# Q and K of a group as one product of 2x4 by 4x4 blocks with 26 multiplications, and every engine's order from a list schedule

## The chip, the cores and the metric

The kernel runs on one NeuronCore of a Trainium2 chip. The metric is the device time of one execution in microseconds (us), as the median of several runs. The kernel before takes 1929.07 us (three runs, 1928.95 to 1929.9).

In the profile the engines are called PE (matrix products), PEld (its weight loads), DVE (VectorE), ACT (ScalarE), POOL (GpSimd) and SP (which only issues DMAs). Matrix products land in PSUM, eight banks of 128 partitions by 512 fp32 values; everything else is in SBUF or in device memory.

## The reference

All data is fp32. There are 128 batches of 128 nodes with 512 features, and two layers:

```python
# layer 0: adj stands for W1 and W2, so C - A is the bias alone
A   = adj @ x                                    # per batch
x   = layernorm(x + max over features of relu(A + b))
# layer 1: eight-head attention, masked where adj == 0
q, k, v = split(x @ w_qkv)                       # 8 heads of 64
attn = softmax(where(adj == 0, -inf, q @ k.T / 8))
o   = (attn @ v) @ w_proj + b_proj
x   = layernorm(x + o + layernorm(o) * gamma + beta)
```

## The kernel before, in words

The 128 batches go in 32 groups of four, so a group has 512 tokens of 512 features. One group after the other passes through these stages, and three or four groups are in work at once:

- Layer 0: `l0_mm` makes adj @ x per batch (one 128x512 product), `l0_max` takes the largest value of each row on DVE, `l0_add` (L302, ACT) adds it to x, `bn` and `finish_stats` make mean and deviation (DVE and POOL), `l0_norm` normalizes (ACT). The result is transposed through a DVE transpose and two DMAs into `x1T`. `l0_beta` (POOL, 128x1024) adds beta and `l0_spill` writes x out for the last residual.
- Q, K and V of a group, and later the projection O, each by Strassen's method. A `Unit` (L163) cuts the 512 tokens and the 512 features into two halves each and makes seven products of half blocks. A product is four matmuls of 128x256. The sums of weight blocks are made once at the start; the four sums of token blocks (`left_sums`, L211) are made per group on POOL, 128x512 each, and `x_sums` (L372) shares one set between Q, K and V. A group has two units for Q and K (`qk_unit`, L378), one for V and one for O: 28 products, 112 matmuls of 128x256.
- Within a unit, products are summed in PSUM where they can be: `snap` (L185, ACT) copies a bank to SBUF, `relay` (L190, ACT) copies a bank into another bank, and `result` (L203, DVE) adds a bank and a copy into the output. Per group that makes, with Q and K alone, six ACT copies and eight DVE additions of 128x512.
- Attention per batch: `scores` (PE), the mask (`softmax_mask`, DVE), the row maximum (`softmax_max`, DVE), eight exponentials (`softmax_exp`, ACT), the division by the row sum (`softmax_div`, L450, one DVE TENSOR_TENSOR of 128x1024 with two inputs in SBUF), a DVE transpose (`pu`), two DMA steps to the transposed probabilities `pT`, and `attend` (PE), copied by ACT to `oT`.
- The tail of a group: `tail_bias` adds the bias to o (POOL, 128x1024), then mean and deviation of o, normalization (ACT), times gamma, plus o, plus x (`tail_inner`, `tail_residual`: three POOL operations of 128x1024 per two batches), mean and deviation again, the last normalization (ACT), and the store.

The order of the work on every engine is the order in which the program issues it (`pin`), written out by hand: PE works on one group's unit while DVE, ACT and POOL prepare the next, and the two units of Q and K, V and O are interleaved product by product so that there is always another product to run while a bank is being copied. Memory comes from pools with two to four buffers to a name.

The lines that matter below are these. L75 is the helper of all matmuls, L78 that of every TENSOR_TENSOR, on DVE and on POOL; L187 is the copy of `snap`; L274 and L276 are in `finish_stats`, L300 in `l0_max`, L418 the mask, L434 the row maximum, L441 the exponentials, L462 the transpose of probabilities, L692 a last normalization on DVE. In the tile names of the page `b_qk`, `b_v`, `b_o` are PSUM banks of the units, `u_qk` and so on the copies, `s_x` and `s_o` the token sums.

Of the kernel before, what the change touches and what calls it, by code (L numbers as in the profile page):

```python
# [1 line left out]

# [7 lines left out]
F32 = mybir.dt.float32  # L10
AF = mybir.ActivationFunctionType
ALU = mybir.AluOpType
AX = mybir.AxisListType


@with_exitstack
def kernel(
# [12 lines left out]

# [6 lines left out]
    GT = G * P  # L55
    HT = GT // 2
    HE = D // 2
    NG = B // G
    NP = H // 2
    Q = 4  # L60
    QS = P // Q
    LA = 10
# [3 lines left out]
    const = ctx.enter_context(tc.tile_pool(name="const", bufs=1))  # L66
    sb = ctx.enter_context(tc.tile_pool(name="sb", bufs=1))
    small = ctx.enter_context(tc.tile_pool(name="small", bufs=4))
    dram = ctx.enter_context(tc.tile_pool(name="dram", bufs=3, space=bass.MemoryType.DRAM))
    psum = ctx.enter_context(tc.tile_pool(name="psum", bufs=1, space=bass.MemoryType.PSUM))  # L70

    pin = tc.keep_in_program_order

    def pe(*args, **kwargs):
        pin(nc.tensor.matmul(*args, **kwargs))  # L75
# [3 lines left out]

    zeros = const.tile([P, 2 * P], F32, name="zeros")
    pin(nc.vector.memset(zeros, 0.0))
    idle = psum.tile([P, 2 * P], F32, tag="b1", name="idle")

    def keep_warm(n):
        for _ in range(n):
            pe(idle, lhsT=zeros[:, :P], rhs=zeros, start=True, stop=True)

    adj_sb = const.tile([P, P], F32, name="adj_sb")  # L90
    pin(nc.sync.dma_start(out=adj_sb, in_=adj))
    bias0 = const.tile([P, 1], F32, name="bias0")
    pin(nc.sync.dma_start(out=bias0, in_=l0_b.unsqueeze(1)))

    def broadcast(queue, name, src):
        t = const.tile([P, D], F32, name=name)
        pin(queue.dma_start(out=t, in_=src.partition_broadcast(P)))
        return t
# [3 lines left out]
    xs, pairs = {}, {}  # L102

    def load(q, *queues):
        tag, bufs = ("o", 3) if 2 <= q <= 4 else ("x", 2)
        pairs[q] = t = sb.tile([P, 2, D], F32, tag=tag, name=f"x_{q}", bufs=bufs)
        for j, queue in enumerate(queues):
            pin(queue.dma_start(out=t[:, j], in_=x[2 * q + j]))
        if not queues:
            pin(nc.sync.dma_start(out=t, in_=x[ds(2 * q, 2)].rearrange("j p d -> p j d")))  # L110
        for j in range(2):
            xs[2 * q + j] = t[:, j]
# [3 lines left out]
    def weight_load(w, src, col1, col2, cols, width):  # L116
        rows = src.rearrange("(d c p) e -> d p c e", d=2, p=P)
        for i, d, col in ((0, 0, col1), (3, 0, col2), (1, 1, col1), (2, 1, col2)):
            pin(
                nc.sync.dma_start(  # L120
                    out=w[:, i, :, ds(cols, width)], in_=rows[d, :, :, ds(col + cols, width)]
                )
            )

    def weight_sums(w, cols, width, *steps):
        t = w[:, :, :, ds(cols, width)]
        b11, b21, b22, b12 = (t[:, i] for i in range(4))
        sums = ((4, b12, b11), (6, b22, b12), (5, b22, t[:, 4]), (3, b21, t[:, 5]))
        for i, left, right in {(): sums, (1,): sums[:1], (2,): sums[1:3], (3,): sums[3:]}[steps]:
            tt(nc.gpsimd, t[:, i], left, right, ALU.subtract)  # L130

    WQK = [P, 7, 2, D]
    wqk = sb.tile(WQK, F32, tag="wqk", name="wqk")
    wv = const.tile([P, 7, 2, HE], F32, name="wv")
    wp = const.tile([P, 7, 2, HE], F32, name="wp")

    load(0, nc.scalar, nc.scalar)
    load(1, nc.sync, nc.sync)
    be_bc = broadcast(nc.scalar, "be_bc", ln_beta)
    weight_load(wqk, w_qkv, 0, D, 0, HE)  # L140
    load(2)
    weight_load(wqk, w_qkv, 0, D, HE, HE)
    load(3)

    warm = small.tile([P, 1], F32, tag="r", name="warm")
    pin(nc.scalar.activation(warm, zeros[:, :1], AF.Identity, bias=zeros[:, :1]))
    keep_warm(3)
    ident = const.tile([P, P], F32, name="ident")
    make_identity(nc, ident)
    mhalf = const.tile([P, 1], F32, name="mhalf")  # L150
    pin(nc.gpsimd.memset(mhalf, -0.5))
# [3 lines left out]
    adjT = const.tile([P, P], F32, name="adjT")  # L155
    pt0 = psum.tile([P, P], F32, tag="po", name="pt0")
    pin(nc.tensor.transpose(pt0, adj_sb, ident))
    pin(nc.vector.tensor_copy(adjT, pt0))
    mask = const.tile([P, P], F32, name="mask")
    pin(nc.vector.tensor_scalar(mask, adj_sb, 0.0, -3.0e38, ALU.is_equal, ALU.mult))  # L160


    class Unit:  # L163

        def __init__(self, name, lefts, mm, out):
            self.name, self.lefts, self.mm, self.out = name, lefts, mm, out
            self.banks, self.snaps = {}, {}  # L170

        def product(self, i):
            bank = {1: 1, 6: 1, 7: 1, 2: 2, 5: 3, 3: 3, 4: 4}[i]
            first = bank not in self.banks
            if first:
                self.new_bank(bank)
            self.mm(self.banks[bank], i - 1, self.lefts[i], first)

        def new_bank(self, bank):
            self.banks[bank] = psum.tile(  # L180
                [P, 2, HT], F32, tag=f"b{bank}", name=f"b{bank}_{self.name}"
            )
            return self.banks[bank]

        def snap(self, k):  # L185
            t = sb.tile([P, 2, HT], F32, tag=f"u{k}", name=f"u{k}_{self.name}")
            pin(nc.scalar.copy(t, self.banks[1]))  # L187
            self.snaps[k] = t

        def relay(self):  # L190

            pin(nc.scalar.copy(self.new_bank(2), self.banks[1]))

        def relayed(self):
            for dst, src in self.places(0, 0, self.banks[2]):
                pin(nc.scalar.copy(dst, src))

        def places(self, half, col, bank):

            out = self.out[half, col]  # L200
            return [(d, bank[:, k]) for k, d in enumerate(out)] if type(out) is list else [(out, bank)]

        def result(self, half, col):  # L203
            bank, k = {(0, 0): (2, 1), (0, 1): (3, 2), (1, 0): (4, 3), (1, 1): (3, 3)}[half, col]
            adds = zip(
                self.places(half, col, self.banks[bank]), self.places(half, col, self.snaps[k])
            )
            for (dst, a), (_, b) in adds:
                tt(nc.vector, dst, a, b, ALU.add)

    def left_sums(name, a11, a12, a21, a22):  # L211
        s = [
            sb.tile([P, 2, HT], F32, tag=f"{name[0]}s{k}", name=f"s{k}_{name}") for k in range(1, 5)
        ]
        return dict(zip((1, 2, 3, 4, 5, 6, 7), (a11, a12, s[3], a22, s[0], s[1], s[2]))), (
            (s[0], a21, a22, ALU.add),
            (s[1], s[0], a11, ALU.subtract),
            (s[2], a11, a21, ALU.subtract),
            (s[3], a12, s[1], ALU.subtract),
        )  # L220

    def run_sums(sums, eng=None):
        for dst, a, b, op in sums:
            tt(eng or nc.gpsimd, dst, a, b, op)

    def weight_stationary(w, cols):
        def mm(bank, i, left, first):
            for k in range(2):
                for c in range(2):
                    pe(  # L230
                        bank[:, k],
                        lhsT=w[:, i, c, ds(cols + k * P, P)],
                        rhs=left[:, c],
                        start=first and k == 0 and c == 0,
                        stop=True,
                        skip_group_check=True,
                    )

        return mm

    def tokens_stationary(w):
        def mm(bank, i, left, first):
            for k in range(2):
                for c in range(2):
                    pe(
                        bank[:, k],
                        lhsT=left[:, c, ts(k, P)],
                        rhs=w[:, i, c],
                        start=first and k == 0 and c == 0,
                        stop=True,  # L250
                        skip_group_check=True,
                    )

        return mm


    NC = 6
    stat_of = {}

    def bn(src, mv, k):  # L260
        st = small.tile([P, 6], F32, tag="st", name=f"st_{k}_{mv.name}")
        pin(nc.vector.bn_stats(st, src))
        pin(nc.vector.bn_aggr(mv[:, k], st))  # L263

    def finish_stats(mv, keys, fused=0):


        n = len(keys)
        if n == 0:
            return  # L270
        part = slice(fused, n)
        sh = small.tile([P, NC], F32, tag="sh", name=f"sh_{mv.name}")
        if n > fused:
            pin(nc.vector.tensor_scalar(sh[:, part], mv[:, part, 0], -1.0, None, ALU.mult))  # L274
# [1054 lines left out]
```

## Time and profile before

| | |
|---|---|
| median of three runs | 1929.07 us |
| span of the profiled execution | 1927.6 us, 1.5 us under the median |
| PE busy | 1915.8 us, 99% of the span |
| DVE busy | 1591.0 us, 83% |
| POOL busy | 1289.5 us, 67% |
| ACT busy | 1054.4 us, 55% |
| device memory | 176 GB/s over the span, DMA engines about two thirds busy |
| period of a group, from the chain of waits | 59.39 us (the same piece begins at 941.09 and 1000.48 us) |

The page gives the busy time of each engine, then the span in 40 slices, then the chain of work that ended last, then groups of equal instructions with the mean duration of one, and the idle time of the engine ahead of them. The timeline lists single instructions: start, duration, engine, line, output and inputs, shape. Its duration of an instruction contains the time that it is held up after it was issued, so that the same instruction can have several durations.

### The profile page before, as it was taken

To read this page: it belongs to the slowest core of one execution; us is meant where nothing else is said; L and a number is where in the kernel's file an instruction comes from. 1 tells how busy PE (TensorE), PEld (TensorE's weight loads), DVE (VectorE), ACT (ScalarE), POOL (GpSimd) and SP (SyncE) were. 2 spreads that over 40 slices of the span, in tenths; PEclk is the share of its full clock that TensorE was granted. 3 is DMA by queue.
4 is the path that set the end of the run, shared out by engine and by line. 5 is a ranking of instruction groups with operands and counts; after the bars stand their busy time and mean duration, and the time that the engine had idled before them with its cause. 6 is when DMAs were issued, how large, how long until landed. Compare 5 with 4: busy or idle time off the path is not lost.

```text
span 1927.6 us, 33369 instructions
## 1 busy us (share of the span) xinstructions
PE 1915.8 (99%) x11539; PEld 1637.9 (85%) x11539; DVE 1591.0 (83%) x2516; ACT 1054.4 (55%) x3093; POOL 1289.5 (67%) x826
## 2 busy tenths in 40 slices
PE   9999999999999999999999999999999999999998
PEld 7888888888888888888888888888888888888885
DVE  6868888888888888888888888888888888888888
ACT  3444655645555556555465564555555655546476
POOL 6444766768667676676676676766767667677658
PEclk9999999999999999999999999999999999999999
DMA  7746667666676666766667756667666676666665
GB/s 228 179 127 165 162 186 191 164 183 158 181 203 158 186 164 180 203 162 178 169 179 189 179 169 180 162 187 198 162 187 158 182 206 158 181 165 182 170 196 177
DMA packets 444936, 341.76 MB, mean 177 GB/s; under 512 B 276832, under 2 KB 378336, under 8 KB 444768
## 3 DMA queue, kind: packets, MB, share of 16 engines
q1 hardware_dynamic: 444336, 338.85, 65.9%
q8 instruction: 91, 1.49, 0.3%
q10 hardware_dynamic: 432, 0.79, 0.1%
q14 instruction: 77, 0.63, 0.1%
HBM read 172.82 MB, written 166.72 MB: 176 GB/s over the span
## 4 chain that ended last, share of the span: by engine, by line
PE 97%; POOL 1%; DMA 1%; DVE 1%; ACT 0%; issue 0%; SPq 0%; POOLq 0%; ACTq 0%
PE b_qk L75 40%; PE b_o L75 19%; PE b_v L75 19%; PE pss L75 6%; PE po L75 6%; PE pa L75 6%; POOL zl L78 0%; DMA x<-in_x_dram 0%; DMA pT<-hop 0%; DVE s L78 0%; POOL rs_mv_last L78 0%; ACT s L441 0%; DMA hop<-pu 0%; PE idle L75 0%; DVE pu L462 0%
## 5 line engine op out<-in xcount | busy, mean ns | idle before, releaser
L75 PE MATMUL b_qk<-s_x,wqk 128*128 128x256 f32 x2048 | 472.8, 379 | 0.0
L75 PEld LDWEIGHTS b_qk<-s_x,wqk 128*128 128x128 f32 x2048 | 389.0, 190 | 53.5 <-DVE xt L323 0.2
L441 ACT ACTIVATE s<-s,nmax 128x128 f32<-128x128 f32 x1008 | 390.2, 391 | 4.5 <-DVE nmax L434 4.5
L75 PE MATMUL b_qk<-x1T,wqk 128*128 128x256 f32 x1536 | 360.5, 381 | 0.1
L276 POOL TENSOR_SCALAR rs_mv<-mv 128x6 f32<-128x6 f32 (+2 forms) x61 | 14.7, 241 | 501.2 <-DVE mv L263 501.2
L75 PEld LDWEIGHTS b_qk<-x1T,wqk 128*128 128x128 f32 x1536 | 289.3, 190 | 43.1 <-issue 1.0
L78 DVE TENSOR_TENSOR s<-s,rec 128x1024 f32<-128x1024 f32 x126 | 282.5, 2242 | 4.3
L78 DVE TENSOR_TENSOR qk<-b_qk,u_qk 128x512 f32<-128x512 f32 x256 | 170.3, 687 | 137.0 <-ACT u_qk L187 83.7
L187 ACT COPY u_qk<-b_qk 128x512 f32<-128x512 f32 x192 | 112.5, 586 | 276.9 <-PE b_qk L75 275.3
L75 PE MATMUL b_v<-wv,s_x 128*128 128x256 f32 x1024 | 236.9, 379 | 0.1
L75 PE MATMUL b_o<-wp,s_o 128*128 128x256 f32 x992 | 229.3, 379 | 0.0
L418 DVE SCALAR_TENSOR_TENSOR s<-pss,mask 128x512 f32<-128x512 f32 x252 | 156.2, 682 | 78.5 <-PE pss L75 78.4
L75 PEld LDWEIGHTS b_v<-wv,s_x 128*128 128x128 f32 x1024 | 194.4, 190 | 27.0 <-DVE qk L78 0.5
L75 PEld LDWEIGHTS b_o<-wp,s_o 128*128 128x128 f32 x992 | 188.3, 190 | 25.8 <-POOL zl L78 0.2
L78 POOL TENSOR_TENSOR z<-z,ga_bc 128x1024 f32<-128x1024 f32 x58 | 162.8, 2807 | 51.0 <-ACT z L285 51.0
L441 ACT ACTIVATION_READ_ACCUMULATOR s<-s,nmax 128x1 f32 x1008 | 190.7, 189 | 0.0
L187 ACT COPY u_v<-b_v 128x512 f32<-128x512 f32 x95 | 55.6, 585 | 246.2 <-PE b_v L75 242.8
L187 ACT COPY u_o<-b_o 128x512 f32<-128x512 f32 x91 | 53.3, 586 | 250.2 <-PE b_o L75 250.2
L78 POOL TENSOR_TENSOR x<-x,be_bc 128x1024 f32<-128x1024 f32 x64 | 178.3, 2787 | 17.5 <-DVE xt L323 16.2
L75 PE MATMUL b_v<-wv,x1T 128*128 128x256 f32 x768 | 176.5, 379 | 0.0
L75 PEld LDWEIGHTS b_v<-wv,x1T 128*128 128x128 f32 x768 | 145.8, 190 | 32.3 <-issue 13.9
L75 PE MATMUL b_o<-wp,oT 128*128 128x256 f32 x744 | 171.1, 379 | 0.0
(142 smaller groups left out, 3305.7 us busy)
## 6 DMA issues: line engine op xcount, KB each, us to landing
hop<-pu SPq DMA_DIRECT2D x128, 512.0 KB, 3.1
pT<-hop SPq DMA_DIRECT2D x512, 128.0 KB, 3.8
spill<-x SPq DMA_DIRECT2D x64, 512.0 KB, 5.2
x<-in_x_dram SPq DMA_DIRECT2D x62, 512.0 KB, 4.5
xhop<-xt SPq DMA_DIRECT2D x248, 128.0 KB, 2.3
x1T<-xhop SPq DMA_DIRECT2D x248, 128.0 KB, 3.9
xr<-spill SPq DMA_DIRECT2D x59, 512.0 KB, 3.6
out_dram<-xr SPq DMA_DIRECT2D x58, 512.0 KB, 4.5
```

The lines of the kernel that those rows point to most:

```text
L75: pin(nc.tensor.matmul(*args, **kwargs))
L78: pin(eng.tensor_tensor(dst, a, b, op))
L187: pin(nc.scalar.copy(t, self.banks[1]))
L276: pin(nc.gpsimd.tensor_scalar(rs[:, :n], mv[:, :n, 1], EPS, None, ALU.add))
L418: nc.vector.scalar_tensor_tensor(s[:, par], pss[b][par], SCALE, mask.unsqueeze(1).to_broadcast([P, NP, P]), ALU.mult, ALU.add,)
L441: nc.scalar.activation(prob[b][:, i], prob[b][:, i], AF.Exp, bias=nmax[b][:, i : i + 1], accum_out=psums[b][:, i : i + 1],)
```

## The change

The change rewrites the program around a planner. What it does:

- Q and K of a group become one product. The tokens are cut into 2 by 4 blocks (two batches of 128 tokens each, by 128 features), the weights of Q and K into 4 by 4 blocks (128 features by 256 outputs). 26 products, each of one 128x256 token block (a sum or a plain block) and one of 26 weight blocks, take the place of the 14 products of half blocks. A product is now two matmuls of 128x256, so a group has 52 instead of 56. The first group makes Q and K plainly with 64 matmuls from the weights as they are.
- The token blocks: 18 sums of 128x256 per group on POOL (`token_sums`). V makes its four sums of 128x512 itself.
- The outputs: a table `NODES` gives for each of 26 steps which product goes into which of eight banks, into which other banks the bank is copied by ACT (`seeds`), whether it is copied to SBUF by ACT for later additions (`adds`), and which of the eight outputs it ends. Per group there are 18 ACT copies of 128x512 for Q and K, eight DVE operations that write the outputs, two DVE additions in PSUM and two POOL additions of 128x512.
- The weight blocks for Q and K are made at the start, by 39 additions of 128x256 on DVE and POOL and six ACT operations.
- `tail_bias` is gone: ACT puts the bias into the banks of O ahead of its products (two copies of 128x512 per group). `l0_add` is gone: the row's constant goes into the shift of the normalization (`finish`, on POOL).
- The division of the softmax is no longer one DVE operation with two inputs. It is eight operations of 128x128 per batch, with a column of reciprocals as pointer scalar: on ACT for batches 0 and 2 of a group, on DVE for batches 1 and 3 (TENSOR_SCALAR).
- V's product 3 (`closing`) comes after O's products 1 and 2, O's product 3 after the third step of Q and K; both add to a bank out of which DVE must have taken `result(1, 1)`.
- Most buffers are single. PE's order is the order in which the program adds the work; the order on DVE, ACT, POOL and SP comes from `Plan.run`, a list schedule over costs written into the program: whenever an engine is free, of the operations that are ready the one that is due first.
- The last group's projection, residual and normalization are written anew with POOL for one half and DVE for the other.

The core of the diff. The change takes these out (of the functions above `qk_unit`, `x_sums`, `left_sums`, `tail_bias`, `l0_add` and the written-out order of the groups go as well):

```diff
-    def softmax_div(b):
-        rec = small.tile([P, H], F32, tag="rec", name=f"rec_{b}")
-        pin(nc.vector.reciprocal(rec, psums.pop(b)))
-        p = prob[b]
-        tt(nc.vector, p, p, rec.unsqueeze(2).to_broadcast([P, H, P]), ALU.mult)
```

It puts these in:

```diff
+NODES = [
+    (((8, 0),), 0, 3, (2,), (), None),
+    (((12, 1),), 2, 6, (), (19,), None),
+    (((14, 2),), 1, 4, (8,), (), None),
+    (((1, 3), (10, 4)), 0, 5, (), (7,), None),
...
+    (((2, 25),), 0, None, (), (), 0),
+]
...
+    def run(self, lead):
...
+            while coming[e] and coming[e][0][0] <= now + 1e-9:
+                _, n, op = heapq.heappop(coming[e])
+                heapq.heappush(ready[e], (op.due, n, op))
+            _, _, op = heapq.heappop(ready[e])
+            op.start = now
+            free[e] = now + op.cost
...
+    def token_sums(g):
...
+        for n, (a, b, s) in enumerate(SUMS):
...
+            plan.add(
+                "POOL",
+                0.74,
+                lambda t=t, c=c, pa=pa, pb=pb, s=s: tt(
+                    GP, t.t[:, c], pa(), pb(), ALU.add if s > 0 else ALU.subtract
+                ),
+                [(ba, ka), (bb, kb)],
+                [(t, c)],
+            )
...
+    def qk_unit(g, phys, between=()):
...
+        for n, (prods, lb, chain, seeds, adds, block_) in enumerate(NODES):
...
+            for tok, w in prods:
...
+                def emit(b=b, w=w, ap=ap, fresh=fresh):
+                    for s in range(2):
+                        mm(halves(b)[:, s], wqk.t[:, w, ts(s, P)], ap(), fresh and s == 0)
+
+                plan.add("PE", 0.862, emit, [(wqk, w), (bt, key)], [b])
...
+                for m in seeds:
+                    nb = bank(phys[NODES[m][1]])
+                    plan.add("ACT", 0.5, lambda b=b, nb=nb: pin(A.copy(nb.t, b.t)), [b], [nb])
+                    banks[m] = nb
+                if adds:
+                    u = snap_buf(range(6))
+                    plan.add("ACT", 0.5, lambda b=b, u=u: pin(A.copy(u.t, b.t)), [b], [u])
+                    snaps[n] = (u, adds)
...
+    class Unit:
+        BANK = {1: 0, 6: 0, 7: 0, 2: 1, 5: 2, 3: 2, 4: 3}
+        RESULT = {(0, 0): (1, 1), (0, 1): (2, 2), (1, 0): (3, 3), (1, 1): (2, 3)}
...
+    DIV = {0: "ACT", 1: "DVE", 2: "ACT", 3: "DVE"}
+
+    def softmax(b, bs):
...
+        plan.add("DVE", 0.17, lambda: pin(V.reciprocal(rec.t, sm.t)), [sm], [rec])
+        for par in range(2):
+
+            def emit(par=par, eng=DIV[b % 4]):
+                for i in range(4 * par, 4 * par + 4):
+                    p, r = flat()[:, i], rec.t[:, i : i + 1]
+                    if eng == "ACT":
+                        pin(A.activation(p, p, AF.Identity, scale=r))
+                    else:
+                        pin(V.tensor_scalar(p, p, r, None, ALU.mult))
+
+            plan.add(
+                DIV[b % 4], 1.15 if DIV[b % 4] == "ACT" else 0.72, emit, [rec, (s, par)], [(s, par)]
+            )
...
+    X, Y = [0, 1, 2, 3], [4, 5, 6, 7]
+    for p in range(NG - 1):
+        a = G * p
+        if p > 0:
+            for j in range(G):
+                attend(a - G + j, Y[j])
+        ks = (*X, *Y)
+        bs = [scores(a + j, ks[2 * j], ks[2 * j + 1]) for j in range(G)]
...
+        v = v_unit(p, X)
+        v.opening()
+        for j in range(G):
+            softmax(a + j, bs[j])
...
+        v.middle()
...
+        v.rest()
...
+            o = o_unit(p - 1, Y)
+            o.product(1)
+            o.snap(1)
+            o.product(2)
+            v.closing()
+            o.result(0, 0)
+            o.middle()
+            o.rest()
...
+        token_sums(p + 1)
...
+            between = {2: [o.closing]}
+        qk_unit(p + 1, phys, between)
+        if p > 0:
+            tails(p - 1)
...
+    for op in plan.run(3.0):
+        op.emit()
```

On DVE the built program has, for a steady group, this order around the first run of divisions: reciprocal of batch 1, two aggregates, eight TENSOR_SCALAR of 128x128 (batch 1), two small operations, the transposes of batches 0 and 1, the two results of V that free its bank for product 3. Around the second run: reciprocal of batch 3, eight TENSOR_SCALAR of 128x128 (batch 3), the transposes of batches 3 and 2, two layer-0 transposes, one statistic, then the two results of O that free its bank for product 3. POOL's order is: two additions to Q and K, then the tail's and O's operations in turn (128x1024 and 128x512), 18 token sums, layer 0's statistics, a residual and a beta addition of 128x1024, the tail's statistics, a second beta addition, V's sums.

## The prediction

> **What bounds the kernel now.** I read the page's busy times and chain first:
>
> ```profile
> PE 1915.8 (99%) x11539; PEld 1637.9 (85%) x11539; DVE 1591.0 (83%) x2516; ACT 1054.4 (55%) x3093; POOL 1289.5 (67%) x826
> ...
> PE 97%; POOL 1%; DMA 1%; DVE 1%; ACT 0%; issue 0%; SPq 0%; POOLq 0%; ACTq 0%
> ```
>
> PE is busy all the time and is the chain. The view of PE's waits has only five entries, all at the two ends (1.2, 0.9, 0.9, 0.4, 0.2 us), so no other engine's delay has reached PE in steady state. Time falls only if PE's work falls, and then only if the others keep up. Hence the second reading, groups and single instructions on DVE and POOL, where the change puts work:
>
> ```profile
> L78 DVE TENSOR_TENSOR s<-s,rec 128x1024 f32<-128x1024 f32 x126 | 282.5, 2242 | 4.3
> L187 ACT COPY u_qk<-b_qk 128x512 f32<-128x512 f32 x192 | 112.5, 586 | 276.9 <-PE b_qk L75 275.3 <-issue 1.6
> ```
>
> The softmax division averages 2.24 us, though one beside an idle POOL takes 1.22 (at 1884.19). The timeline says why:
>
> ```profile
> 951.24 2.35 POOL L78 TENSOR_TENSOR xr<-xr,z 128x1024 f32<-128x1024 f32 x1
> ...
> 951.86 2.81 DVE L78 TENSOR_TENSOR s<-s,rec 128x1024 f32<-128x1024 f32 x1
> ...
> 953.55 3.34 POOL L78 TENSOR_TENSOR x<-x,be_bc 128x1024 f32<-128x1024 f32 x1
> ```
>
> DVE's operation, issued at 951.86, ends at 954.67, 1.1 us after POOL's `xr` ended (953.59): it waited out POOL's whole instruction. POOL's next then took 3.34 instead of 2.35. They take turns by instruction. With several queued:
>
> ```profile
> 19.96 0.76 DVE L78 TENSOR_TENSOR s_x<-x1T 128x512 f32<-128x512 f32 x1
> 20.75 1.64 DVE L78 TENSOR_TENSOR s_x<-s_x,x1T 128x512 f32<-128x512 f32 x1
> 22.31 1.75 DVE L78 TENSOR_TENSOR s_x<-x1T 128x512 f32<-128x512 f32 x1
> ```
>
> Beside POOL's 128x512 weight sums (1.27 alone) the second and third take 1.64 and 1.75: one for one. Does a TENSOR_SCALAR, the form the change puts in, do this too?
>
> ```profile
> 1872.04 0.17 DVE L274 TENSOR_SCALAR sh_mv_last<-mv_last 128x2 f32<-128x2 f32 x1
> ...
> 1879.13 1.26 POOL L78 TENSOR_TENSOR zl<-zl,ga_bc 128x512 f32<-128x512 f32 x1
> ...
> 1879.59 0.82 DVE L274 TENSOR_SCALAR sh_mv_last<-mv_last 128x2 f32<-128x2 f32 x1
> ```
>
> The same 128x2 takes 0.17 beside an idle POOL, and 0.82 when POOL runs; it ends at 1880.41, POOL at 1880.39. (One-column ones, as L300, never wait: 211 to 216 ns in all 128.)
>
> **What the Trainium skill says.** "SBUF — State Buffer", section "Who interferes with whom": DVE and GpSimd share a port pair under an exclusive lock held for a whole instruction; a DVE instruction with two SBUF inputs contends with GpSimd's reads, one in a 2-port mode with any GpSimd instruction. The first two fences agree. "VectorE: DVE Perf Modes", section "Mode 2×_2P — use both read ports for one tensor": a single-source fp32 TENSOR_SCALAR from SBUF to SBUF runs at two elements per cycle through both ports. The trace agrees: 128x128 (`mask`) takes 0.218, 128x2 0.17, so 126 columns cost 0.05 us. So taking the second tensor away doesn't take the lock away.
>
> **The change, part by part.** Basis: the profiled 1927.6 us (the median is 1.5 more).
>
> 1. *PE.* A product of four matmuls takes 1.725 us (eight records, 1.73 in the chain), 0.4313 each. Q and K: before 32x56 = 1792, after 31x52+64 = 1676; one warming matmul less; one 128x512 product more (0.86). 117x0.4313 - 0.86 = **-49.6 us**. The period goes from 59.39 to 57.67.
>
> 2. *ACT.* Starts 0.48 apart for a copy, 0.385 for an exponential, 0.71 for a normalization; a plain 128x128 0.29 (start of the exponential to its accumulator's read). Per group 30 copies 14.4, 32 exponentials 12.3, 16 divisions 4.6, 12 normalizations 8.5: 39.8 of 57.7. Hidden by PE's work, but for one turn: after step n0 the bank of n2 needs PE-to-ACT 0.26 and 0.61 from copy to use, with only n1 (0.862) between: 0.1 at least, and ACT has layer 0's normalizations ahead, which wait for POOL. I take 0.3 (bounds 0.1 and 0.6), x31 = **+9**.
>
> 3. *POOL.* 128x1 takes 0.19, 128x512 1.27, so a 128x256 sum is estimated at 0.73. Per group 18 sums 12.8, eight of 128x512 9.8, eight of 128x1024 (2.4) 19.2, two additions 2.5, three statistics 6: 50 of 57.7 (40.7 of 59.4 before, windows view). The removed 128x1024 bias (2.85, one per half group) is counted. Fits, thinly.
>
> 4. *DVE.* Masks 8x0.61, maxima 4x1.12, 12 statistics 0.8 each, 18 additions 0.61, transposes 7.4, row maxima 3, 16 TENSOR_SCALAR at 0.18 (0.13 from L300's start to the next one's, and 0.05), reciprocals 0.8: about 45 of 57.7. Fits if nothing waits.
>
> 5. *The divisions on DVE against POOL.* From a group's first attend, PE: attend to 3.65, scores to 7.4, V 1 and 2 to 10.9, then V's product 3 is due at 24.7 and O's at 35.9. DVE runs from 4.9 without a gap: masks to 9.8, four maxima, one result, four row maxima, two statistics, to about 19.1; batch 1's divisions free to 20.5; two transposes to 23.2; V's two results to 24.4. Slack for V's product 3: about 0.5. POOL is then in its token sums (0.73 each). One for one, a turn is 0.73+0.13, eight are 6.9 instead of 1.4: 5.4 late, **PE stands 4.5 to 5** at V's product 3. Later, batch 3's eight meet two 128x1024 operations (2.4 each, the first perhaps half over), after which POOL itself waits for DVE's statistics and the rest run free: 3.3 to 4.8 late; behind them are four transposes, a statistic and O's two results, with 0.3 slack: **PE stands 3**. PE's order is fixed, so nothing fills this. 7.5x29 groups = **+217** (bounds: 0 if the lock passes to DVE more than once per turn, 11 per group if the first run meets 128x1024 operations).
>
> 6. *Ends.* Head: +1 (-2 to +6), Q and K of group 1 start behind their token sums. Tail: once O's last results but one are out, about 35 us into the last group, POOL has in order 12 operations at 1.25, 12 small statistics at 1.5 and four at 0.8, some 37 us; with 4 for gaps, normalizations and store the end is at about 78, PE's at 54: 24 us beyond PE instead of 8 (1919.67 to 1927.6). **+16** (+8 to +20).
>
> DMA traffic is the same and its list order follows; device memory is not the limit.
>
> Sum: 1927.6 - 49.6 + 9 + 217 + 1 + 16 = 2121; as a median 2122. I say 2120.
>
> **The rivals.**
> - *Divisions hidden* (chance 0.33): the lock wait stays below the slack, because DVE with a full queue keeps the port over several of its short instructions. Place: the 128x128 TENSOR_SCALARs of batches 1 and 3; price nothing; it decides if eight take under about 2 us. Then 1904, median **1906**, 1893 to 1922. For it: the short ones hold the port only some 0.1 us, and no run here shows eight in a row. Against it: the head's turns.
> - *All hidden* (0.07): also n2 without a stall and a shorter tail: 1927.6 - 49.6 + 9 = 1887, about **1888**.
> - *Partly hidden* (0.05): two of three turns are skipped, 1 to 2 us per group: 1906 + 45 = **1951**, 1920 to 1975.
> - *The saving isn't there*: excluded, matmuls of one form and counted in the built program.
>
> **How the numbers follow.** The forecast (0.55) has its own range of 2000 to 2210: 3.5 to 10.5 us per group. A difference of under 0.2% (1925.2 to 1932.9) can't be told from none. Faster is the first two rivals and a part of the third: 0.41; same 0.03; slower 0.56. For 8 in 10 the range leaves out the second rival, the first's lowest few and the forecast's upper end: 1893 to 2210.
>
> **What would show it.** Right: 128x128 TENSOR_SCALAR on DVE means about 0.8 us or more (free: 0.2 to 0.27); PE's waits name `result` outputs of V and O (DVE) at 4 to 5 and 3 us, some 30 times each; the period is about 65; PE's busy time about 1866; the chain has DVE and POOL in it. Wrong: TENSOR_SCALAR near 0.25, period near 58. A PE wait on ACT's copies would mean that part 2 was mis-sized; one beyond 20 us of PE's end at the tail bears out part 6.

## The result and the profile after

The changed kernel takes **2102.89 us** (four runs, 2098.84 to 2104.45) against 1929.12: 1.0896 times as long, interval 1.0881 to 1.0912. The forecast was 2120. The profiled execution has a span of 2097.0 us, 169.4 more than that of before. Busy times and chain of the page:

```profile
PE 1932.3 (92%) x11307; PEld 1614.5 (77%) x11307; DVE 1523.7 (73%) x2906; ACT 1339.5 (64%) x3893; POOL 1568.2 (75%) x1634
...
PE 60%; DVE 26%; ACT 5%; DMA 3%; issue 3%; POOL 2%; SPq 1%; ACTq 0%; DVEq 0%; POOLq 0%
```

The matmuls have become fewer (11307 records for 11539), yet PE is busy 16.5 us longer, and DVE stands in the chain with 26%. PE's waits (total, times, longest), of which before had five at the two ends:

```profile
PE k L315 <- DVE v L309: 75.3, 29, 3.1
PE k L315 <- ACT u L752: 57.8, 31, 4.3
PE k L315 <- POOL hl L309: 3.6, 1, 3.6
PE k L315 <- ACT k L748: 2.5, 7, 1.2
```

There are two waits per group: one for a result of V (DVE), one for an ACT copy out of a bank of Q and K. The first, in the timeline (start, duration):

```profile
955.37 5.21 DVE L1043 TENSOR_SCALAR s<-s,rec 128x128 f32<-128x128 f32 x8
955.63 1.41 POOL L309 TENSOR_TENSOR hl<-x1T,hl 128x256 f32<-128x256 f32 x2
957.00 0.72 POOL L309 TENSOR_TENSOR hl<-hl,hl 128x256 f32<-128x256 f32 x1
...
963.73 2.97 PE L315 MATMUL k<-wv,hl 128*128 128x256 f32 x8 [2.66 <-DVE v L309]
```

The eight divisions take 5.2 us beside token sums that follow each other every 0.69 us; two transposes and V's results come after them, and PE stands 2.66 us. The view by windows (length; busy PE, PEld, DVE, ACT, POOL; then PE's granted clock, the share of full speed that PE was given) shows what follows:

```profile
963.73:968.00 4.27, 4.27 (x12) 3.44 (x13) 3.31 (x9) 2.19 (x10) 1.22 (x2) 0.60 0.62 225
968.00:990.00 22.00, 22.00 (x102) 19.18 (x102) 15.39 (x36) 14.76 (x26) 17.49 (x22) 1.00 0.96 246
```

After the wait PE runs at a clock of 0.60 for 4.3 us. The second wait, some 30 us later:

```profile
994.34 0.69 DVE L312 SCALAR_TENSOR_TENSOR qk<-k,u 128x512 f32<-128x512 f32 x1 [0.52 <-PE k L315]
995.06 0.59 ACT L752 COPY u<-k 128x512 f32<-128x512 f32 x1 [4.47 <-DVE qk L312]
995.54 0.81 ACT L472 ACTIVATE z<-o,sh,rs 128x512 f32<-128x512 f32 x1
996.26 1.06 ACT L752 COPY u<-k 128x512 f32<-128x512 f32 x2
996.89 0.48 PE L315 MATMUL k<-x1T,wqk 128*128 128x256 f32 x1 [1.73 <-ACT u L752]
```

ACT has stood 4.47 us in front of a copy, until a DVE operation was done; then it takes a normalization, and only then the copy that PE waits for. From the program: the first copy is that of step 14. Six buffers go round, and it gets the one that step 1's copy holds until the result of step 19.

### The profile page after: what moved, and what is told of

The parts are those of the page before. It is cut to its first block, busy times and chain, and to the rows that moved or that the text cites. A ratio compares the mean times of both kernels' runs of the same rounds, so it can differ in the third digit from the quotient of the medians.

```text
span 2097.0 us, 35142 instructions
## 1 busy us (share of the span) xinstructions
PE 1932.3 (92%) x11307; PEld 1614.5 (77%) x11307; DVE 1523.7 (73%) x2906; ACT 1339.5 (64%) x3893; POOL 1568.2 (75%) x1634
## 4 chain that ended last, share of the span: by engine, by line
PE 60%; DVE 26%; ACT 5%; DMA 3%; issue 3%; POOL 2%; SPq 1%; ACTq 0%; DVEq 0%; POOLq 0%
PE k L315 60%; DVE s L1043 7%; DVE nm L1015 5%; DVE am L419 3%; DMA x<-in_x_dram 3%; DVE st L430 2%; DVE pu L1053 2%; DVE v L309 2%; SPq L320 1%; ACT s L1024 1%; ACT z L472 1%; DVE qk L312 1%; ACT u L752 1%; POOL x L309 1%; ACT k L748 1%
## 5 line engine op out<-in xcount | busy, mean ns | idle before, releaser
L315 PE MATMUL k<-hl,wqk 128*128 128x256 f32 x2232 | 520.2, 382 | 1.4 <-ACT k L748 1.4
L315 PEld LDWEIGHTS k<-hl,wqk 128*128 128x128 f32 x2232 | 423.6, 191 | 67.7 <-issue 9.4
L1024 ACT ACTIVATE s<-s,nm 128x128 f32<-128x128 f32 x1024 | 395.7, 390 | 3.5 <-DVE nm L1015 3.2
L315 PE MATMUL k<-wv,hl 128*128 128x256 f32 x1024 | 268.8, 410 | 78.9 <-DVE v L309 75.3
L752 ACT COPY u<-k 128x512 f32<-128x512 f32 x341 | 190.1, 589 | 215.6 <-DVE qk L312 142.9
L315 PEld LDWEIGHTS k<-wv,hl 128*128 128x128 f32 x1024 | 204.8, 203 | 146.8 <-DVE v L309 87.3
L315 PE MATMUL k<-x1T,wqk 128*128 128x256 f32 x992 | 252.5, 388 | 58.9 <-ACT u L752 57.8
L315 PEld LDWEIGHTS k<-x1T,wqk 128*128 128x128 f32 x992 | 187.6, 193 | 99.0 <-ACT u L752 70.3
L315 PE MATMUL k<-wp,so 128*128 128x256 f32 x992 | 241.4, 393 | 0.1
L309 POOL TENSOR_TENSOR hl<-x1T 128x512 f32<-128x512 f32 (+1 forms) x250 | 216.9, 874 | 28.1 <-PE k L315 16.9
L1043 DVE TENSOR_SCALAR s<-s,rec 128x128 f32<-128x128 f32 x512 | 226.8, 512 | 1.2
L861 ACT COPY u<-k 128x512 f32<-128x512 f32 x189 | 109.1, 577 | 102.0 <-PE k L315 96.4
```

What stands on the lines that cost most here:

```text
L309: pin(eng.tensor_tensor(dst, a, b, op))
L315: pin(PE.matmul(dst, lhsT=lhsT, rhs=rhs, start=start, stop=True, skip_group_check=True))
L752: plan.add("ACT", 0.5, lambda b=b, u=u: pin(A.copy(u.t, b.t)), [b], [u])
L861: plan.add("ACT", 0.5, lambda: pin(A.copy(u.t, b.t)), [b], [u])
L1024: A.activation(flat()[:, i], flat()[:, i], AF.Exp, bias=nm.t[:, i : i + 1], accum_out=sm.t[:, i : i + 1],)
L1043: pin(V.tensor_scalar(p, p, r, None, ALU.mult))
```

## The experiments

The theory: DVE's TENSOR_SCALARs wait for POOL's instructions one by one (first wait), the buffer rotation makes the second, the slowed clock is a consequence. The rival: DVE and ACT are merely late with more and shorter work. e1 to e4, e8 and e10 are one run each; e5, e6, e7 and e9 are four. The traces show the same order of instructions on PE, ACT and POOL in e1 and e2 as in the changed kernel, and on DVE too but for the division itself.

**e1: two TENSOR_TENSOR in place of eight TENSOR_SCALAR.**

```diff
+                if eng == "DVE":
+                    p = flat()[:, 4 * par : 4 * par + 4]
+                    r = rec.t[:, 4 * par : 4 * par + 4]
+                    tt(V, p, p, r.unsqueeze(2).to_broadcast([P, 4, P]), ALU.mult)
+                    return
...
-                        pin(V.tensor_scalar(p, p, r, None, ALU.mult))
...
```

> Edit: on DVE the eight TENSOR_SCALAR of 128x128 of a batch become two TENSOR_TENSOR of 128x512 with two SBUF inputs; every engine's order stays as in the changed kernel. Theory (port taken by turns, one POOL instruction per DVE instruction): two waits in place of eight, so a batch's division takes about 2 x (0.7 + 0.7) = 2.8 us instead of 5.1, PE's wait on V's result falls from 2.6 us to 0.3 or less per group, PE is no longer slowed after it, and the time falls by 29 x (2.3 + 1.7) = 116, to about 1985. Rival (DVE is merely late with its work; the form of the division doesn't matter): the wait stays over 2 us and the time over 2080.

Measured: 2008.37 us. A group of instructions and a wait of PE:

```profile
L309 DVE TENSOR_TENSOR s<-s,rec 128x512 f32<-128x512 f32 x128 | 119.8, 974 | 1.2
```
```profile
PE k L315 <- ACT k L748: 23.4, 33, 1.6
```

The wait on V is gone, though this form also takes turns (0.97 us on average, 0.68 at least). A new one of some 0.8 us per group appeared, on the seed copy of step n2, 23 us in all, about what the result lies above the 1985 expected. The wait on the ACT copy stays (59.2 us in all).

**e2: the same eight instructions, without the second port.**

```diff
+        junk = small("junk", H)
...
-                        pin(V.tensor_scalar(p, p, r, None, ALU.mult))
+                        pin(V.tensor_scalar(p, p, r, None, ALU.mult, ALU.add, accum_out=junk.t[:, i : i + 1]))
```

> Edit: the same eight TENSOR_SCALAR on DVE at the same places, but in the form that also writes a sum of its elements (never read), which the Trainium skill (SBUF - State Buffer, Who interferes with whom) excludes from the 2-port modes; orders unchanged. Theory: each takes about 0.25 to 0.35 us whatever POOL does, eight about 2 to 2.5 us, PE's wait on V's result is gone or under 0.3 us, time about 1985. Rival (many short DVE instructions are slow in themselves): eight still take over 4 us and the time stays near 2100.

Measured: 2012.98 us. The groups show the form under another name, with a small second instruction each:

```profile
L1044 DVE TENSOR_SCALAR_CACHE_REDUCE s<-s,rec 128x128 f32<-128x128 f32 x512 | 141.7, 342 | 1.2
L1044 DVE DVE_READ_ACCUMULATOR s<-s,rec 128x1 f32 x512 | 42.4, 83 | 0.0
```

The wait on V is gone here as well, with as many short divisions at the same places in the same orders. So number and place of the instructions are not the cause; the form that waits for POOL is. The result is 28 us over the 1985 expected, because the other wait remains and is longer: 70.3 us for 57.8, and the clock is still slowed after it.

**e3: a buffer of its own for step 1's copy.**

```diff
-                    u = snap_buf(range(6))
+                    u = buf("so0", [P, 512]) if n == 1 else snap_buf(range(6))
```

> Edit: the copy that step 1 of Q and K leaves for step 19 gets a buffer of its own (a token-sum buffer of O, unused at that time) instead of one of six in turn. Theory for the second wait of PE (1.86 us per group on an ACT copy): the copy of step 14 gets the buffer that step 1's copy holds until step 19's result, so ACT stands in front of the copy that PE needs next; with a buffer of its own that wait goes, 31 x 1.86 = 58 us, to about 2045. Rival (ACT is late because of a normalization that it takes first): the wait stays at 1 us or more and the time over 2075. The wait on V's result stays at 2.6 us in both.

Measured: 2017.18 us, 28 less than the theory said. The ACT wait has left the list; the wait on V (77.0 in all) stays. ACT still takes the normalization between the same two copies (its order differs at four places only), so the normalization was not the cause. Of the 28, 24 lie in PE's busy time: 1907.9 for 1932.3. The other 4 are the difference between the median of the changed kernel's runs and its profiled one. Two of the waits in the timeline of e3 show how the clock enters:

```profile
987.50 1.99 PE L315 MATMUL k<-wv,hl 128*128 128x256 f32 x8 [2.66 <-DVE v L309]
1048.22 3.52 PE L315 MATMUL k<-wv,hl 128*128 128x256 f32 x8 [2.66 <-DVE v L309]
```

The same product after the same wait takes 1.99 us or 3.52. The Trainium skill ("TensorE: Matmul & The Clock Gate", section "Part 1: The HAM clock gate (the "warmup" mystery)") says that PE's clock is halved after an idle window of about 3.4 us, given back after a busy one, and that the windows run freely, whenever the kernel starts. The trace agrees on the windows: its slow stretches ahead of PE's end are 3.41 us long or twice that, and begin on one grid of 3.41 us. It differs on what is idle. These are windows of that grid, one of the first wait and two of the second:

```profile
983.09:986.50 3.41, 1.75 (x9) 1.19 (x7) 3.41 (x6) 3.30 (x16) 3.23 (x5) 1.00 0.02 5
1044.53:1047.94 3.41, 1.03 (x5) 0.57 (x3) 3.41 (x6) 3.41 (x18) 2.52 (x4) 1.00 0.19 78
1047.94:1051.35 3.41, 3.13 (x7) 2.52 (x8) 2.32 (x7) 2.74 (x12) 0.00 (x0) 0.50 0.83 302
```

The first wait falls across a border of the grid, PE is busy 1.75 us of the window, and the clock stays at 1.00 in the next. The second falls into one window, PE is busy 1.03 of 3.41 us, and the next runs at 0.50. So a wait well under 3.4 us is enough. In the changed kernel and in e1 to e4 (from 60 us to PE's end, counting windows at full clock), every window in which PE was busy for a share of 0.42 or less was followed by one at half clock, and none from 0.46 up. A wait of 1.72 us leaves at least 0.49 and never cost clock; one of 2.66 us does when most of it falls into one window.

**e4: O's product 2 made twice** (the second overwrites the first), to fill PE's wait.

```diff
             o.product(2)
+            o.again(2)
             v.closing()
```

(`again`, left out here, makes the product's four matmuls anew in the same bank.)

> Edit: O's product 2 is made twice in a row (the second overwrites the first), 1.7 us of PE work more per group, exactly where PE stands waiting for V's result; all other orders unchanged. Theory: after PE has stood for 2.7 us its granted clock is 0.5 to 0.7 for about 4 us (1.7 us lost per group); with the repeat it stands only 0.9 us, the clock stays at 1.0, and in spite of 30 x 1.7 us more work the time falls by about 50, to 2050. Rival (the slow stretch has another cause): the time stays at 2100, or rises to 2150 if the wait was not idle at all.

Measured: 2071.76 us: 51.8 us more PE work (30 products of 1.725), and 31 us less time. The wait on V fell from 75.3 to 26.8, and beyond the added work PE's busy time fell by 30.8 us (1932.3 + 51.8 - 1953.3). The direction was right; the size (50) was not. The loss of 1.7 us per group that it reckoned with occurs in part of the groups only, and the other wait still slows PE: at 982.72 a wait of 2.2 us is followed by a step of 2.07 us, while after waits of 1.72 it takes 1.13.

**e5, e6, e7: both repairs, with three ways to divide.** e5 is e2 and e3, e6 is e1 and e3; apart from the division, the orders in both are those of e3. e7 is e3 with this:

```diff
-    DIV = {0: "ACT", 1: "DVE", 2: "ACT", 3: "DVE"}
+    DIV = {0: "ACT", 1: "ACT", 2: "ACT", 3: "ACT"}
```

> Edit: both e2 and e3: divisions on DVE in the form without the second port, and a buffer of its own for step 1's copy. Theory (PE's two waits per group and the slowed clock after them are the whole loss in steady state): PE busy is back at about 1866, waits 10 us in all, tail 20 us after PE's end: 1897 to 1905, under the 1929 of before. Rival (a third wait is behind them, such as step n2 behind layer 0's normalizations, as the prediction's part 2 has it): 0.3 to 0.8 us per group more, 1907 to 1925; the added effects of e2 and e3 alone would give 1927.

Measured: 1908.06 us, 0.9888 of before (0.9874 to 0.9903): 1.1% under the old kernel, and under both kernels.

```profile
PE 1874.4 (98%) x11307; PEld 1590.2 (83%) x11307; DVE 1430.7 (75%) x3418; ACT 1339.1 (70%) x3893; POOL 1565.2 (82%) x1634
```

It is 3 us over the theory's range and inside the rival's, but the rival's third wait is not there: PE waits for seed copies 0.5 us in all, and its largest wait (V) is 4.8 us in all. PE is busy 8 us more than 1866, and that is not the clock: the granted clock is 1.00 until PE's last matmul. What these 8 us are stays open. Together the repairs gain 189 us of span, 22 more than e2 (86) and e3 (82) taken singly: each of these left one wait, after which PE was still slowed (28 us in either, 43 in the changed kernel, none in e5), and in e2 that wait was 12 us longer.

> Edit: both e1 and e3: two TENSOR_TENSOR per batch on DVE and a buffer of its own for step 1's copy. Theory: as the run before, but the divisions still hold POOL up (each DVE operation by some 0.65 us), so that layer 0's normalizations are late and step n2 waits 0.7 us per group on ACT (23 us, as in e1): about 1920. Rival (no further cost of the port): as fast as the run before within 3 us.

Measured: 1938.88 us (1.0052, 1.0037 to 1.0067), with this wait, as in e1:

```profile
PE k L315 <- ACT k L748: 21.4, 27, 1.3
```

It stands at step n2 as before. The mechanism held, the sum was 19 short: PE's busy time was 15 over 1866 and single waits on V, O and the token sums came to 12. The rival, no further cost, is out: the time is 31 us over e5's, and POOL is busy 1611.2 us for 1565.2, with the same work in the same order; only DVE's 128 divisions with two SBUF inputs differ.

> Edit: all divisions on ACT, none on DVE, and a buffer of its own for step 1's copy; the list schedule orders all engines anew. Theory: no DVE instruction takes the port, ACT's busy time rises by 256 x 0.29 = 74 us to 1425 of about 1905 (75%), which it can hold: no wait on V's result, 1895 to 1915. Rival (ACT, in order, is then too late with banks and copies): waits on ACT copies of 1 us and more per group, over 1930.

Measured: 1942.16 us (1.0068, 1.0051 to 1.0084). Both missed: the rival's ACT waits of 1 us per group are not there, and yet the time is over its 1930 and not under the theory's 1915. PE's listed waits come to some 30 us, short ones on O's results (9.9) ahead; the chain has ACT in it with 29%, and from 1870 to 1925 PE is busy 47 of 55 us. The list schedule has changed the orders on DVE, ACT and POOL here, so what part of it costs most stays open.

**e8: the division alone, in the kernel before.**

```diff
-        tt(nc.vector, p, p, rec.unsqueeze(2).to_broadcast([P, H, P]), ALU.mult)
+        for i in range(H):
+            pin(nc.vector.tensor_scalar(p[:, i], p[:, i], rec[:, i : i + 1], None, ALU.mult))
```

> Edit: the kernel before with this one part of the change alone: its DVE division of 128x1024 becomes eight TENSOR_SCALAR of 128x128 with a pointer scalar, orders as written. Theory (turns with POOL): a group has 32 of them, and where POOL is at work each waits for one of its operations (1.27 to 2.4 us): mean of one 0.7 us or more, DVE's busy time per group over 60 us of 59.4, so DVE becomes the bound: 2000 to 2350. Rival (short instructions slip between POOL's): 0.18 to 0.27 each, less than the 2.24 per batch of before, time 1929 within 0.5%.

Measured: 2191.61 us. Groups, then timeline:

```profile
L455 DVE TENSOR_SCALAR s<-s,rec 128x128 f32<-128x128 f32 x1008 | 675.0, 741 | 4.5
```
```profile
1023.56 2.35 POOL L78 TENSOR_TENSOR z<-z,o 128x1024 f32<-128x1024 f32 x1
1024.75 8.95 DVE L455 TENSOR_SCALAR s<-s,rec 128x128 f32<-128x128 f32 x8
1025.99 2.41 POOL L78 TENSOR_TENSOR xr<-xr,z 128x1024 f32<-128x1024 f32 x1
1028.36 2.36 POOL L78 TENSOR_TENSOR x<-x,be_bc 128x1024 f32<-128x1024 f32 x1
1030.67 2.35 POOL L78 TENSOR_TENSOR o<-o,bp_bc 128x1024 f32<-128x1024 f32 x1
```

Four POOL operations pass while eight divisions, which undisturbed start every 0.20 us, get through: 8.95 us. Four of the divisions wait out one of these operations each, one slips in behind the first, and the last three run when POOL has no further work. This part alone costs the old kernel 262 us, more than the whole change.

**e10: the same in the form without the port.** `accum_out` added as in e2, in the kernel before.

> Edit: the kernel before with its division as eight TENSOR_SCALAR of 128x128 in the form that also writes a sum (never read), without the second port. Theory: 0.25 to 0.35 each beside POOL too, no PE wait, time within 0.4% of before's 1929. Rival (e8's 2192 came of 32 short DVE instructions per group, whatever port they use): over 1960.

Measured: 1931.72 us; the group:

```profile
L457 DVE TENSOR_SCALAR_CACHE_REDUCE s<-s,rec 128x128 f32<-128x128 f32 x1008 | 278.8, 342 | 4.5
```

As many short divisions, no cost to speak of (0.1%). Of the two forms, only the one that waits for POOL costs e8's 262 us.

**e9: the tail relieved on POOL**, on top of e5. One small operation of each one-batch statistic of the last two groups goes to DVE in place of two on POOL, and for every second batch of the last group but one its three 128x512 operations:

```diff
+        if n == 1 and rows is None:
+            plan.add(
+                "DVE",
+                0.17,
+                lambda: stt(sh.t[:, :1], mv.t[:, part, 0], -1.0, rs.t[:, :1], ALU.mult, ALU.mult),
+                [rs, *at],
+                [sh],
+            )
+            return [(rs, sh, 0)]
...
-            plan.add(
-                "POOL", 1.28, lambda with_=with_, op=op: tt(GP, z(), z(), with_(), op), [zk, rd], [zk]
-            )
+            eng, e, cost = ("DVE", V, 0.72) if b % 2 else ("POOL", GP, 1.28)
+            plan.add(
+                eng, cost, lambda with_=with_, op=op, e=e: tt(e, z(), z(), with_(), op), [zk, rd], [zk]
+            )
```

> Edit: e5 with the last two groups' tail relieved on POOL: for every second batch its three 128x512 operations go to DVE, and two of four small operations of each one-batch statistic become one on DVE. Theory (part 6: POOL's queue sets the end, 20 us beyond PE in e5): about 8 x 1.25 + 12 x 0.5 = 14 us less POOL work in that queue, of which half or so is seen, because the statistics still pass between DVE and POOL: the end comes 6 to 10 us earlier, 1898 to 1902. Rival (the end hangs on the chain of the last batch, not on POOL's queue): within 3 us of e5's 1908.

Measured: 1901.15 us, 0.9854 of before (0.9838 to 0.9871), 7 less than e5. The end is now 7 us after PE's last matmul and not 20; part of that is eaten by two new waits of PE in the tail (3.1 and 2.2 us).

## Why the prediction was right

The direction was right, and so was the mechanism of its main term: DVE's divisions wait for POOL one by one, until PE stands at a result of V. That the total came within 1% was luck in good part: the port was priced at 217 us, its waits came to 75.3, and what was missing was made up by a wait on ACT and a longer busy time of PE that the sum did not have. Step by step against the 169.4 us between the spans:

- *Part 1, PE.* The count and price hold: a matmul record of 128x256 is 379 to 383 ns on average in e5, 379 to 381 before, and e5's PE busy time is 41.4 us under that of before, where 49.6 was forecast; the other 8 stay open.
- *Part 2, ACT.* The forecast wait at n2 was 9 us in all. All waits on seed copies came to 2.5, those at n2 to 1.4, at both ends of the run; in the groups between, n2 did not wait. The place was well seen: as soon as POOL was held up, n2 waited in nearly every group (e1, 0.8 us each). What the step overlooked was the order of ACT's copies against the buffers that they go into: 57.8 us, shown by e3.
- *Parts 3 and 4.* POOL is busy 48.8 us of a group of 64.4 (50 forecast), DVE 47.1 including its waits for the port. Neither is the bound. (Part 3's 18 sums at 0.73 make 13.1, not 12.8.)
- *Part 5, the port.* This is the mis-sized term: +217 forecast, 75.3 measured as wait. With all that follows from it, clock included, taking the port away was worth 86 us (e2), or 107 with the buffer repaired (e3 to e5). On V, 4.5 to 5 forecast and 2.6 measured: eight divisions took 5.1 us and not 6.9, because a turn costs DVE the 0.69 of POOL's sums and nothing more and the first turn was half over; and DVE had 1.0 us of slack and not 0.5 (5.1 less 1.4 less the wait of 2.66). On O, 3 forecast and none measured:

```profile
966.78 0.73 POOL L309 TENSOR_TENSOR hl<-hl,hl 128x256 f32<-128x256 f32 x1 [4.23 <-PE k L315]
...
968.37 1.97 DVE L1043 TENSOR_SCALAR s<-s,rec 128x128 f32<-128x128 f32 x8
```

  Batch 3's divisions took 1.97 us. POOL had stood 4.23 us because its next sum goes into a buffer that PE still had to read for V (PE's first wait made that late), so that it had only 128x256 and small operations to offer when they ran. The step took POOL to be past its sums and in 128x1024 operations.
- *Not in the prediction: the slowed clock.* PE's busy time is 66 us over the 1866 that were forecast. 43 of them are the clock: PE was busy for 86 us at half of it, nearly all in windows after waits of 2.0 us and more. Of the other 23, e5 still has 8, without any slow clock; most of the rest are the ends of matmuls ahead of the 79 places where PE stood, which no next matmul overlaps. e4 gets 31 back by filling one wait with useless work.
- *Part 6, ends.* The end lies 20 us after PE's last matmul (24 forecast), 12 more than before (16 forecast); e9 shows that POOL's queue set it. (The forecast's addends, 35, 37 and 4, make 76 and not 78, which leaves 22.) The head has one wait of 3.6 us where the forecast had 1.

Sum of the measured: -49.6 + 75.3 + 57.8 + 66 + 12 = 161.5; the other 8 are small waits. The forecast's sum was 193. Without the overlooked buffer wait and PE's 66 us, 46 us would be left, or 1973, and the mis-sized port term would have shown: the forecast's own range began at 2000. Of the signs that it named, the period (64.4 us) and the wait on V in nearly every group came; the wait on O did not, the mean of a TENSOR_SCALAR was 0.51 us and not 0.8, PE's busy time was 1932 and not 1866, and the wait on ACT's copies was the sign that it gave for a mis-sized part 2. The rival "divisions hidden" named 1906 for the case without the port's cost; with the port's cost taken out and the buffer repaired, e5 came to 1908.

## What to carry to other kernels

Before you cut an SBUF-to-SBUF operation on DVE into many short ones, count the instructions and not the bytes: where POOL is at work, each one in a 2-port form can cost a whole POOL instruction. A wait of PE of about 1.9 us or more can cost another 1.7 us, half of a 3.41 us window, in clock, so ask for each bank's turn what is queued ahead of the releasing instruction, on its engine and for its buffer. A kernel with fewer matmuls gains only when those queues are shown to fit: here a forecast saving of 49.6 us became a loss of 174, and two small edits made it a gain of 21.

## What the runs showed of the hardware

- A DVE TENSOR_SCALAR in the form that waits for POOL hardly slows POOL: POOL's 128x1024 operations take 2.35 to 2.41 us on average in e8, 2.35 to 2.37 in e10, and its busy time falls from 1289.5 us before to 1181.1. A TENSOR_TENSOR with two SBUF inputs does: 113 us over 126 of them in the kernel before, since without it (e10) POOL is busy 1176.4.
- The turns are one for one nearly always while POOL has work: in the run of divisions at 955.37 of the changed kernel each of the eight ends about 0.1 us after another POOL sum. In the run at 1024.75 of e8, four wait out one operation each, and one slips in behind another in the same turn.
- The TENSOR_SCALAR with a sum as second output takes 0.34 us and is followed by a small read of 0.08; one starts every 0.27 us whatever POOL does, against 0.20 for the other form undisturbed. The Trainium skill ("SBUF — State Buffer", section "Who interferes with whom") excepts this form from the 2-port modes; e2 and e10 agree.
